# Layer 3 attention of a four-layer network: written order, one side piece per step, router on VectorE

## Chip, cores and metric

The kernel runs on one core of a Trainium2 chip, in fp32. The metric is the device time of one execution in microseconds. A core has TensorE (PE in the profile, its weight loads PEld), VectorE (DVE), ScalarE (ACT), GpSimd (POOL) and SyncE (SP, which issues most DMAs).

## What is computed

The network has four layers on x of shape [8, 256, 32, 32]. The change touches the third layer's attention and the routing of its mixture of experts (layers are counted from 0):

```python
# attention, per sample: N = 1024 tokens, D = 256, 8 heads of 32
qkv = layernorm(t) @ qkv_w.T + qkv_b
t2 = square(q @ k.T * 32**-0.5 + 5.0)
attn = t2 / sum(t2, axis=-1)
t = t + (attn @ v) @ proj_w.T + proj_b
# experts: 8 experts, each token goes to its best two
logits = layernorm(t) @ router_w.T
w, e = top_k(softmax(logits), 2); w = w / max(sum(w), 1e-12)
tokens = layernorm(t)
t = t + tokens + sum(w[i] * (gelu(tokens @ w1[e[i]] + b1[e[i]]) @ w2[e[i]] + b2[e[i]]) for i in (0, 1))
```

The denominators of the attention are had in closed form: the sum over m of (s_m + 5)^2 with s linear in k needs only the 32x32 matrix G = k k^T of a head (and the sum of k), then a product of G with q (Gq), a product with q and a sum over the head (D). Its inverse is Exp(-Ln(D)).

## The kernel before

Each layer is a generator; a layer's weights are loaded while the one before it still runs. Instructions are written in program order, and the compiler's tile scheduler then orders each engine's queue by priority and readiness. What is `pinned` keeps its place in program order. A pool with `bufs` buffers hands a tile out again when its last readers are done, and the first writer of the new tile waits for that.

`fast3` (attention) handles the 8 samples one after the other. For each one there are 32 steps (half of the queries, block of four heads, key tile of 128). A step does in TensorE four score products, one for each head of 32 channels, in four row strips of the array (L2686), into two PSUM tiles S of two banks each; in ScalarE two squares of 128x1024, from S to e (L2692); in TensorE the products of e with v of the step before (L2670), into the bank A. After 8 steps A times the inverse denominator goes to o (L2675), and after 16 the output projection of half a sample follows (L2681 adds it to x). PSUM has 8 banks: S has three buffers of two banks, A two buffers of one.

Beside the steps of sample b run, spread by `spread` over 33 calls: the routing of sample b-1 (`Routes.route`), and the norm, the transposes (xn), the projections q, k, v and the denominators of sample b+1. All these draw their PSUM from S as well (`pair`). In sample 0 `Routes.fill` also writes fill rows to the sorted lists in DRAM. `Routes.sort`, after each group of three samples, scatters rows by expert with GpSimd (L1026).

`Routes.route` normalizes the tokens (L1003 to L1019), stores them (L2390), adds them to x in GpSimd (L2391) and stores that too (L2392); transposes them on TensorE (L2398), takes the logits on TensorE (`mo_l`, 16 products with 8 columns), and then finds ranks, weights and places on VectorE. x has three buffers: that of sample b, of b+1, and of the one that is routed or loaded (L2570).

`fast3e` (experts) works on pairs of 128-row tiles. It first writes 16 half pairs beside the routing of the last sample:

```python
by_time([[0, 1, some(all_pairs, lead)], [1, 1.1, routing]])
```

In `by_time` each stream has a due time, a stride and a generator; the stream that is due first goes next.

Of the kernel before, what the change touches and what calls it, by code (L numbers as in the profile page):

```python
# [18 lines left out]
B = 8  # L19
# [878 lines left out]
class Fast:  # L898
# [123 lines left out]

    def scatter(self, group, after=(), **args):


        made = self.nc.gpsimd.indirect_dma_start(**args)  # L1026
        self.pinned(made)
        ins = made.ins
        self.tc.declare_no_dep(ins, group=group, reason="rows of their own")
        self.tc.add_to_no_dep_group(group, ins)  # L1030
        self.wait_for(ins, after)
        self.groups.setdefault(group, []).append(ins)
# [9 lines left out]
    def pinned(self, *ins):  # L1042
        for i in ins:
            self.tc.keep_in_program_order(i)

# [1263 lines left out]
class Routes:  # L2309
# [28 lines left out]
    def load(self, wp):  # L2338

        net, nc = self.net, self.net.nc  # L2340
        self.wr = net.load(wp, "l3f_wr", "(k p) o -> p k o", p=P)
# [17 lines left out]
    def fill(self):  # L2359
# [8 lines left out]
        for g, so in enumerate(self.sorteds):  # L2368
            self.fills[g] = []
            for lo in range(0, TILES[g], 26):  # L2370
# [5 lines left out]
                self.net.pinned(ins)  # L2376
# [3 lines left out]
    def route(self, b, x, ones, pair):  # L2380
# [8 lines left out]
        yield from net.token_norm_steps(xn, x, two)  # L2389
# [3 lines left out]
        yield  # L2393
        xk = ones.tile([P, KC, N], F32, tag="xn", name="mo_xk")
        for c in range(KC):
            ps = pair("mo_xT").rearrange("p h n -> p (h n)")
            for t in range(NT):
                nc.tensor.transpose(ps[:, bass.ts(t, P)], xn[:, t, bass.ts(c, P)], net.ident)  # L2398
            nc.vector.tensor_copy(xk[:, c, :], ps)
            yield  # L2400

        pr = two.tile([P, NT, E8], F32, tag="pr", name="pr")
        for t4 in range(0, NT, 4):
            ps = pair("mo_l")[:, 0]
            for i in range(4):
                net.linear(ps[:, bass.ts(i, E8)], xk, self.wr, bass.ts(t4 + i, P), slice(0, E8))
            nc.vector.tensor_copy(pr[:, t4 : t4 + 4], ps[:, : 4 * E8].rearrange("p (t e) -> p t e", e=E8))
            if not t4:
                yield
        red = two.tile([P, NT], F32, tag="red", name="red")  # L2410
        nc.vector.tensor_reduce(red, pr, AX.X, ALU.max)
        nc.vector.tensor_tensor(pr, pr, each(red), ALU.subtract)
        yield
# [11 lines left out]
        nc.vector.tensor_tensor(eq, other, mine, ALU.is_equal)  # L2425
        nc.vector.tensor_tensor(eq, eq, self.before.unsqueeze(1).to_broadcast([P, NT, E8, E8]), ALU.mult)
# [6 lines left out]
        for i in range(2):  # L2433
# [3 lines left out]
            nc.vector.tensor_reduce(weigh[:, i], tmp, AX.X, ALU.add)  # L2437
        nc.vector.tensor_tensor(red, weigh[:, 0], weigh[:, 1], ALU.add)
# [5 lines left out]
        yield  # L2444

        ps = pair("mo_n")[:, 0]
# [10 lines left out]
        for t in range(NT):  # L2457
            nc.vector.tensor_tensor(place[:, t], cnt[:, 0, t], carry, ALU.add)
            nc.vector.tensor_tensor(carry, carry, cnt[:, 1, t], ALU.add)
        yield  # L2460
# [59 lines left out]
def fast3(net, io):  # L2520
# [4 lines left out]
    with ExitStack() as ctx, ExitStack() as tok, ExitStack() as att, ExitStack() as bef:  # L2525
# [3 lines left out]
        def pair(name):  # L2529
            return net.lent["pair"](name) if not own else own["S"].tile([P, 2, HF], F32, tag="S", name=name)  # L2530

        def bank(name):
            return pair(name)[:, 0]
# [31 lines left out]
        xs, xns, qs, ks, vs, rs = ({} for _ in range(6))  # L2565

        def norm(b):
            x = xs[b] = xpool.tile([P, NT, C], F32, tag="x", name="x")

            (nc.sync if b else nc.scalar).dma_start(out=halves(x), in_=tokens(io.src[b]))  # L2570
            yield
            xt = one.tile([P, NT, C], F32, tag="xt", name="xt")
            yield from net.token_norm_steps(xt, x, norms, b > 0)
            yield
            xn = xns[b] = one.tile([P, KC, N], F32, tag="xn", name="xn")
            for c in range(KC):
                ps = pair("xn")
                for t in range(NT):
                    nc.tensor.transpose(ps[:, t // 4, bass.ts(t % 4, P)], xt[:, t, bass.ts(c, P)], net.ident)
                nc.vector.tensor_copy(xn[:, c, :], ps.rearrange("p h n -> p (h n)"))  # L2580
                yield
            nc.gpsimd.tensor_tensor(x, x, bo.unsqueeze(1).to_broadcast([P, NT, C]), ALU.add)

        def projections(b):
            xn = xns.pop(b)
            for d, w, bias, name in ((qs, wq, bq, "q"), (ks, wkk, bk, "k")):
                d[b] = own["two"].tile([P, KC, N], F32, tag=name, name=name)
                for c in range(KC):
                    ps = pair("qk")
                    for h in range(2):  # L2590
                        net.linear(ps[:, h], w, xn, bass.ts(c, P), bass.ts(h, HF))
                    nc.scalar.activation(d[b][:, c, :], ps.rearrange("p h n -> p (h n)"), AF.Identity, bias=bias(c))
                    yield
            v = vs[b] = own["two"].tile([P, NT, C], F32, tag="v", name="v")
            for t4 in range(0, NT, 4):
                ps = pair("v")
                for i in range(4):
                    net.linear(ps[:, i // 2, bass.ts(i % 2, C)], xn, wv, bass.ts(t4 + i, P), slice(0, C))
                nc.vector.tensor_copy(
                    v[:, t4 : t4 + 4].rearrange("p t c -> p (t c)"), ps.rearrange("p h n -> p (h n)")  # L2600
                )
                yield


            kt = own["k1"].tile([P, NT, KC, P + 4], F32, tag="kt", name="kt")
            nc.gpsimd.memset(kt[:, :, :, P], 1.0)
            for t4 in range(0, NT, 4):
                ps = pair("kT")
                for i in range(4):
                    for c in range(KC):  # L2610
                        nc.tensor.transpose(
                            ps[:, i // 2, (i % 2) * C + c * P : (i % 2) * C + (c + 1) * P],
                            ks[b][:, c, bass.ts(t4 + i, P)], net.ident,
                        )
                nc.vector.tensor_copy(
                    kt[:, t4 : t4 + 4, :, :P], ps.rearrange("p h (i c n) -> p (h i) c n", c=KC, n=P)
                )
                yield
            G = bank("G").rearrange("p (c n) -> p c n", c=KC)
            for c in range(KC):  # L2620
                for t in range(NT):
                    nc.tensor.matmul(
                        G[:, c, : P + 1], lhsT=kt[:, t, c, :P], rhs=kt[:, t, c, : P + 1],
                        start=(t == 0), stop=(t == NT - 1),
                    )
            gm = own["k2"].tile([P, KC, P + 4], F32, tag="gm", name="gm")
            nc.vector.tensor_tensor(gm[:, :, : P + 1], G[:, :, : P + 1], heads.to_broadcast([P, KC, P + 1]), ALU.mult)
            yield
            prod = one.tile([P, KC, N], F32, tag="xt", name="prod")
            r = rs[b] = own["two"].tile([P, KC, N], F32, tag="r", name="r")  # L2630
            for c in range(KC):
                ps = pair("Gq")
                for h in range(2):
                    nc.tensor.matmul(
                        ps[:, h], lhsT=gm[:, c, :P], rhs=qs[b][:, c, bass.ts(h, HF)], start=True, stop=True
                    )
                nc.vector.scalar_tensor_tensor(
                    prod[:, c, :], ps.rearrange("p h n -> p (h n)"), gm[:, c, P : P + 1], qs[b][:, c, :],
                    ALU.add, ALU.mult,
                )  # L2640
                yield
            for c in range(KC):
                ps = pair("D")
                for h in range(2):
                    nc.tensor.matmul(
# [592 lines left out]
```

## Time and profile before

| | us |
|---|---|
| median of 3 runs | 4171.47 (4164.15 to 4185.4) |
| profiled execution, its own time | 4178.96 |
| its span, first to last instruction | 4177.1 |
| attention of sample 0, first score product to the first one of the next sample (about) | 2819.65 to 2943 |
| attention of samples 1 to 6 | 2943 to 3708.8 |
| attention of sample 7 | 3708.8 to 3798.8 |
| experts, then checks of ranges | 3800 to 4177 |

Times in the trace count from the span's start. A row of the costliest groups gives line, engine, operation, tiles (out<-in), shape and count, then busy time and mean duration in ns, then the engine's idle time just before and what ended it. An fp32 product of TensorE leaves two records[...], so four heads are eight. Ends of TensorE's records overlap the next record's start.

### The profile page before, as it was taken

What the parts mean: (1) busy time and instruction counts of PE and PEld (TensorE: products, weight loads), DVE (VectorE), ACT (ScalarE), POOL (GpSimd) and SP (SyncE); (2) the same over time, 40 slices, a digit from 0 to 9 for tenths busy, and PEclk for the clock granted to TensorE, in tenths of its full rate; (3) what the DMA queues carried; (4) which work ended last, traced back from release to release, by engine and by line L of the source; (5) the groups of instructions that cost most, each with busy time, mean ns of one, the idle gap of its engine ahead of it and who ended that gap; (6) DMA issues with size and microseconds to landing.
All of it is one profiled execution on the core that took longest, in us unless ns stands there. A gap on an engine that the chain in (4) does not pass through costs nothing. (4 is left out here: it accounts for less than half of the span.)

```text
span 4177.1 us, 51736 instructions
## 1 busy us (share of the span) xinstructions
PE 3826.0 (92%) x19430; PEld 1887.8 (45%) x19430; DVE 2298.4 (55%) x3994; ACT 2260.1 (54%) x3030; POOL 566.3 (14%) x646
## 2 busy tenths in 40 slices
PE   8999999999878787789999969989899999999987
PEld 3323333333334444454444526653344444346986
DVE  2398798798896489942222356841232333324445
ACT  4556555555553367734334346516566556666554
POOL 0000000000000000000000013430000050124753
PEclk9999999999998889889999979999999999999998
DMA  3313223223131568720000013430700040136676
GB/s 100 113 43 124 90 73 120 88 74 109 62 107 47 185 246 291 264 73 21 21 21 29 22 56 109 142 121 11 219 31 31 9 145 31 37 111 195 202 233 219
DMA packets 210069, 441.13 MB, mean 106 GB/s; under 512 B 22281, under 2 KB 132828, under 8 KB 197396
## 3 DMA queue, kind: packets, MB, share of 16 engines
q1 hardware_dynamic: 186708, 386.17, 28.1%
q0 software_dynamic: 19440, 46.45, 3.3%
q10 hardware_dynamic: 3664, 5.11, 0.4%
q8 instruction: 157, 2.57, 0.3%
q14 instruction: 100, 0.82, 0.1%
HBM read 282.30 MB, written 162.28 MB: 106 GB/s over the span
## 5 line engine op out<-in xcount | busy, mean ns | idle before, releaser
L2692 ACT ACTIVATE e<-s,five 128x1024 f32<-128x1024 f32 x512 | 539.3, 1111 | 280.0 <-PE s L2686 279.2
L1249 DVE SCALAR_TENSOR_TENSOR a<-hp,w_f_vec,a 128x961 f32<-128x961 f32 (+1 forms) x496 | 608.7, 1233 | 115.3 <-ACT a L1242 106.7
L2686 PE MATMUL s<-q,k 32*128 32x512 f32 x2048 | 349.1, 644 | 16.3 <-ACT e L2692 12.1
L1401 ACT ACTIVATE e<-s 128x1024 f32<-128x1024 f32 x256 | 250.2, 1023 | 79.4 <-PE s L1395 62.8
L2670 PE MATMUL A<-e,v 128*32 128x512 f32 x2048 | 279.0, 609 | 0.0
L1355 DVE TENSOR_TENSOR sum<-sum,e 128x1024 f32<-128x1024 f32 x192 | 230.6, 1220 | 87.2 <-ACT e L1401 87.2
L78 PE MATMUL pi<-xn,w_l_wpi 128*128 128x512 f32 x512 | 249.0, 629 | 19.2 <-ACT v L1283 10.0
L1359 PE MATMUL A<-e,va 128*32 128x512 f32 x2048 | 263.0, 610 | 0.0
L2686 PEld LDWEIGHTS s<-q,k 32*128 32x128 f32 x2048 | 111.4, 184 | 179.4 <-issue 96.2
L1395 PE MATMUL s<-q,k 32*128 32x512 f32 x1024 | 181.2, 650 | 2.5 <-ACT e L1401 2.5
L78 PEld LDWEIGHTS pi<-xn,w_l_wpi 128*128 128x128 f32 x512 | 96.7, 199 | 161.9 <-issue 118.2
L2839 PE MATMUL h<-xk,w 128*128 128x128 f32 x1192 | 150.7, 281 | 19.0 <-DVE xk L2825 19.0
L1706 PE MATMUL acc<-wt,z 128*64 128x192 f32 (+4 forms) x1344 | 128.9, 334 | 42.4 <-DVE wt L1761 42.0
L1026 POOL DMA_INDIRECT res<-y,to x149 | 148.4, 996 | 106.6 <-DVE y L2863 47.7
L2839 PEld LDWEIGHTS h<-xk,w 128*128 128x128 f32 x1192 | 148.3, 197 | 24.1 <-DVE xk L2825 19.3
L2808 ACT COPY w<-w_l3f_w 128x512 f32 x149 | 92.6, 625 | 119.6 <-PE h L2839 116.3
L1440 ACT ACTIVATE hp<-pi,pib 128x512 f32<-128x512 f32 x128 | 87.2, 690 | 127.3 <-PE pi L78 127.2
L1310 POOL MEMSET thrice<- 32x128 f32 x32 | 6.3, 196 | 1021.7 <-PE pe L1326 1021.6
L2859 PE MATMUL y<-w_l3f_w,hid 128*128 x596 | 142.8, 382 | 0.3 <-ACT hid L2845 0.3
L1026 POOL DMA_INDIRECT so<-xl,rows x128 | 129.9, 1015 | 93.0 <-issue 51.0
L1706 PEld LDWEIGHTS acc<-wt,z 128*64 128x64 f32 x1344 | 97.7, 151 | 89.5 <-DVE wt L1761 60.1
L1359 PEld LDWEIGHTS A<-e,va 128*32 128x32 f32 x2048 | 57.6, 111 | 174.2 <-issue 172.9
(407 smaller groups left out, 6966.5 us busy)
## 6 DMA issues: line engine op xcount, KB each, us to landing
row<-shifts SPq DMA_DIRECT2D x144, 512.0 KB
x<-d SPq DMA_DIRECT2D x31, 1024.0 KB
xs<-so SPq DMA_DIRECT2D x73, 260.0 KB
so<-zero SPq DMA_DIRECT2D x5, 3380.0 KB
thrice<-vimg SPq DMA_DIRECT2D x64, 256.0 KB
gated<-st SPq DMA_DIRECT2D x32, 512.0 KB
hc<-gated SPq DMA_DIRECT2D x32, 512.0 KB
xl<-mox SPq DMA_DIRECT2D x64, 256.0 KB
```

The costliest lines, as they stand in the source:

```text
L78: self.nc.tensor.matmul(ps, lhsT=w[:, i, m], rhs=src[:, i, cols], start=(i == 0), stop=(i == k - 1))
L1026: made = self.nc.gpsimd.indirect_dma_start(**args)
L1249: nc.vector.scalar_tensor_tensor(to, fr, taps(t_), to, ALU.mult, ALU.add)
L1355: nc.vector.tensor_tensor(half, half, e[j], ALU.add)
L1359: nc.tensor.matmul(state["A"][32 * h : 32 * h + 32, c, :], lhsT=vas[b][:, kt, c, 32 * h : 32 * h + 32], rhs=e[h // 2][:, h % 2, :], start= ...
L1395: nc.tensor.matmul(ss[h // 2][:, h % 2], lhsT=ks[b][32 * h : 32 * h + 32, bass.ts(kt, P)], rhs=qs[b][32 * h : 32 * h + 32, bass.ts(gq, HF) ...
L1401: nc.scalar.activation(es[i][j], ss[j], AF.Exp, scale=SCALE)
L1706: nc.tensor.matmul(acc[o, a * IMG : e * IMG], lhsT=zs[b][:, c, t, :], rhs=wt[:, c, (a - lo) * IMG : (e - lo) * IMG], start=False, stop=(t ...
L2670: nc.tensor.matmul(A[32 * h : 32 * h + 32], lhsT=v[:, kt, c * P + 32 * h : c * P + 32 * h + 32], rhs=e[:, h, :], start=first, stop=last,)
L2686: nc.tensor.matmul(ss[h // 2][:, h % 2], lhsT=k[32 * h : 32 * h + 32, c, bass.ts(kt, P)], rhs=q[32 * h : 32 * h + 32, c, bass.ts(hh, HF)], ...
L2692: nc.scalar.activation(e[:, 2 * j : 2 * j + 2], ss[j], AF.Square, scale=SCALE, bias=five)
L2839: nc.tensor.matmul(ps[:, j, m], lhsT=ws[j][:, k, bass.ts(m, P)], rhs=xk[:, j, k], start=(k == 0), stop=(k == KC - 1),)
```

## The change

It does these things.

- S belongs to the scores alone. A has one buffer, and the freed bank X takes every other product of the loop, in pieces of one bank (`bank`). Evictions are of 128x512 instead of 128x1024.
- The four heads are issued in the order 2, 3, 0, 1 (`LATEST`).
- Attention runs over all 256 steps in one loop. `run(i, beside)` issues what is due in step i of routing, norms, loads, fills and sorts ahead of the values; after the values comes either half of an output projection or what is due of `parts` (projections, denominators, transposes).
- The due times are written by hand. The norm and the load of x run two samples ahead of the attention, the projections one.
- In the loop `in_order` adds, for TensorE, VectorE and ScalarE, a dependency from each instruction to the one before it on its engine, so that the queue is the written order.
- The router's logits come from VectorE: for each of 8 token tiles and 8 experts a product of 128x256 with a sum. The router's weights are for that copied to all partitions (`f3_wr`, 1 MB).
- Fill DMAs wait for the last square of their step (`anchor`).
- Before the loop, sample 1 is also normalized and transposed; behind it the last routing has stride 0.26.

The diff, cut to its core:

```diff
+    def token_norm_pieces(self, dst, x, pool):
...
+        for t in range(n):
+            nc.vector.bn_stats(st[:, t, :], x[:, t, :])
+            nc.vector.bn_aggr(mv[:, t, :], st[:, t, :])
+            if t % 2:
+                yield
+        yield
+        self.pinned(nc.scalar.activation(r[:, 0], mv[:, :, 1], AF.Ln, bias=self.eps5))
+        self.pinned(nc.scalar.activation(r[:, 0], r[:, 0], AF.Exp, scale=-0.5))
+        nc.vector.scalar_tensor_tensor(r[:, 1], mv[:, :, 0], -1.0, r[:, 0], ALU.mult, ALU.mult)
+        yield
+        for t in range(n):
+            nc.vector.tensor_scalar(dst[:, t, :], x[:, t, :], r[:, 0, t : t + 1], r[:, 1, t : t + 1], ALU.mult, ALU.add)
+            if t % 2:
+                yield
...
+    def in_order(self, *engines):
+        traced = self.nc.cur_bb.bb.instructions
+        start = len(traced)
+        yield
+        info = mybir.DependencyInfo(mybir.DependencyClass.NoSync, mybir.DependencyReason.DATA)
+        for engine in engines:
+            last = None
+            for i in traced[start:]:
+                if i.engine == engine:
+                    if last is not None:
+                        self.tc.add_manual_dep(i, last.name, info, reason="as planned")
+                    last = i
...
-        yield from net.token_norm_steps(xn, x, two)
+        yield from net.token_norm_pieces(xn, x, two)
         nc.sync.dma_start(out=self.normed[b], in_=xn)
         nc.gpsimd.tensor_tensor(x, x, xn, ALU.add)
         nc.sync.dma_start(out=self.sums[b], in_=x)
...
+        for t in range(NT):
+            for e in range(E8):
+                nc.vector.scalar_tensor_tensor(
+                    junk, xn[:, t, :], 1.0, self.wr[:, e, :], ALU.mult, ALU.mult, accum_out=pr[:, t, e : e + 1]
+                )
+                if e % 2:
+                    yield
...
+        def fetch(b):
+            x = xs[b] = xpool.tile([P, NT, C], F32, tag="x", name="x")
+            (nc.sync if b else nc.scalar).dma_start(out=halves(x), in_=tokens(io.src[b]))
...
+        def attention(beside, parts):
+            steps = [(b, hh, c, kt) for b in range(B) for hh in range(2) for c in range(KC) for kt in range(NT)]
...
+                if last:
+                    nc.vector.tensor_tensor(os[b][:, c, cols], A, rs[b][:, c, cols], ALU.mult)
+                    if c == KC - 1:
+                        projects.extend((i + 2 + t2 // 2, b, hh, t2) for t2 in (0, 2))
+            for i, (b, hh, c, kt) in enumerate(steps):
+                ss = [own["S"].tile([P, 2, HF], F32, tag="S", name="s") for _ in range(2)]
+                for h in LATEST:
+                    nc.tensor.matmul(
+                        ss[h // 2][:, h % 2], lhsT=ks[b][32 * h : 32 * h + 32, c, bass.ts(kt, P)],
+                        rhs=qs[b][32 * h : 32 * h + 32, c, bass.ts(hh, HF)], start=True, stop=True,
+                    )
+                e = es[i] = own["e"].tile([P, NH, HF], F32, tag="e", name="e")
+                for j in range(2):
+                    anchor[:] = [nc.scalar.activation(e[:, 2 * j : 2 * j + 2], ss[j], AF.Square, scale=SCALE, bias=five)]
+                run(i, beside)
+                if i:
+                    values(i - 1)
+                if projects and projects[0][0] <= i:
+                    project(*projects.pop(0)[1:])
+                    for d in parts:
+                        d[0] += d[0] <= i
+                else:
+                    run(i, parts)
+        LATEST = (2, 3, 0, 1)
+        STEPS, anchor = 4 * NT, []
+        def products(b):
+            yield from projections(b)
+            left = denominators(b)
+            for i, _ in enumerate(left):
+                yield
+                if b + 1 < B and 3 <= i < 7:
+                    turned(b + 1, (i - 3) // 2, (i - 3) % 2)
+                    yield
...
-        own["S"], own["A"] = io.pool(att, "f3s", 3, PSUM), io.pool(att, "f3v", 2, PSUM)
+        own["S"], own["A"] = io.pool(att, "f3s", 3, PSUM), io.pool(att, "f3v", 1, PSUM)
+        fetch(1)
...
+        own["X"] = io.pool(att, "f3o", 1, PSUM)
+        for b in range(B):
+            at = STEPS * b
+            if b + 1 < B:
+                parts.append([at + (3 if b else 0), 0.92, products(b + 1)])
+            if b + 2 < B:
+                beside.append([at + 8, 1, later(1, (fetch(n) for n in (b + 2,)))])
+                beside.append([at + 10, 0.5, norm(b + 2)])
+            if b:
+                beside.append([at + 3, 0.48, routed(b - 1)])
+            if b == 0:
+                beside.append([at + 10, 9, routes.fill(anchor)])
             if b == B - 1:
-                bef.close()
+                beside.append([at + 5, 2, loads()])
+        for g, (first, last) in enumerate(GROUPS[:-1]):
+            beside.append([STEPS * (last + 1), STEPS / (1 + NT * (last - first)), routes.sort(g)])
+        with net.in_order(mybir.EngineType.PE, mybir.EngineType.DVE, mybir.EngineType.Activation):
+            attention(beside, parts)
+        by_time(beside + parts)
...
-        by_time([[0, 1, some(all_pairs, lead)], [1, 1.1, routing]])
+        by_time([[0, 1, some(all_pairs, lead)], [1, 0.26, routing]])
...
+    d["f3_wr"] = np.tile(i["L3_ffn_router_w"].reshape(1, E8 * C), (P, 1))
```

## The prediction

> **What bounds the kernel now.** I first read busy time by engine and by slices on the page, then the costliest groups.
>
> ```profile
> span 4177.1 us, 51736 instructions
> PE 3826.0 (92%) x19430; PEld 1887.8 (45%) x19430; DVE 2298.4 (55%) x3994; ACT 2260.1 (54%) x3030; POOL 566.3 (14%) x646
> ...
> L2692 ACT ACTIVATE e<-s,five 128x1024 f32<-128x1024 f32 x512 | 539.3, 1111 | 280.0 <-PE s L2686 279.2
> ...
> L2686 PE MATMUL s<-q,k 32*128 32x512 f32 x2048 | 349.1, 644 | 16.3 <-ACT e L2692 12.1
> ...
> L2670 PE MATMUL A<-e,v 128*32 128x512 f32 x2048 | 279.0, 609 | 0.0
> ```
>
> The loop is the lines L2686, L2692 and L2670: 256 steps, 32 for each of 8 samples. ScalarE waits 279 us for scores, TensorE only 12 us for ScalarE, so TensorE is the bound. Busy time in stretches, of five steady samples (2 to 6), the last sample, and the first 46 us of the experts:
>
> ```profile
> core 0: us, PE busy (x) PEld busy (x) DVE busy (x) ACT busy (x) POOL busy (x), PEclk, DMA share, GB/s
> 3082.00:3708.80 626.80, 623.14 (x3703) 259.42 (x3703) 205.73 (x589) 383.24 (x385) 107.16 (x96) 1.00 0.16 54
> 3708.80:3798.80 90.00, 89.54 (x594) 33.09 (x594) 23.86 (x78) 69.97 (x71) 52.41 (x64) 0.98 0.53 161
> 3800.00:3846.00 46.00, 40.88 (x287) 37.74 (x288) 28.50 (x90) 26.34 (x58) 18.38 (x22) 0.96 0.70 241
> ```
>
> TensorE is busy 99% at full clock, VectorE 33%. A steady sample takes 626.8/5 = 125.4 us. What fills it shows TensorE's timeline (start, duration, line, count of records):
>
> ```profile
> 3105.01 1.46 PE L2686 MATMUL s<-q,k 32*128 32x512 f32 x8
> 3106.40 1.06 PE L2670 MATMUL A<-e,v 128*32 128x512 f32 x8
> 3107.40 1.23 PE L2686 MATMUL s<-q,k 32*128 32x512 f32 x8
> ...
> 3143.36 1.14 PE L2686 MATMUL s<-q,k 32*128 32x512 f32 x8
> 3144.43 1.07 PE L2670 MATMUL A<-e,v 128*32 128x512 f32 x8
> 3145.42 3.70 PE L78 MATMUL qk<-xn,w_l_wq 128*128 128x512 f32 x8
> ```
>
> I use distances from start to start, since ends overlap. A score group whose four heads run together takes 1.07 us (3143.36 to 3144.43), one that starts in two parts 1.39 (3105.01 to 3106.40) or up to 2; values take 0.99. Adding these distances over the 626.8 us gives, for each sample: scores 41.0 (1.28 a step), values 32.8, routing 6.4 (transposes 2.05, logits 3.76, counts 0.6), the rest 45.1 (q and k 14.5, v 7.3, transposes of x and of k 2.05 each, G 3.8, Gq and D 3.83 each, output projection 7.7).
>
> **What the Trainium skill says.** "TensorEngine Tiling (Array Packing)", Key Properties: tiles of the array run in parallel; the 1.07 us for four heads agrees. Its PSUM Bottleneck section says that eviction can become the bound after such a speedup. "Perfetto Trace Analysis", Matmuls: independent groups should rotate through PSUM banks so that an eviction overlaps the next group. That holds before (side work shares three pairs of banks with the scores) and no longer after, where it has one bank; no trace of before shows the cost. "TensorE: Matmul & The Clock Gate", Architectural detail: VectorE and ScalarE are strict queues, so an instruction that waits holds all behind it. The trace agrees: VectorE once stood 15.5 us for a load of x in sample 1, and TensorE lost 11.2 us there.
>
> **The change, part by part (per steady sample).**
>
> Scores. They own the three pairs, each step writes one group, and the heads of the later-freed pair come first, so that all four start together: 32 x 1.07 = 34.2 instead of 41.0, **-6.8**. Values unbroken: 32 x 0.99 = 31.7, **-1.1**.
>
> Router. 16 transposes and 16 logit products leave TensorE: 2.05 + 3.76, **-5.8**. VectorE gets 64 products with a sum. Layer 2 has the same form:
>
> ```profile
> 2435.82 0.42 DVE L2127 SCALAR_TENSOR_TENSOR junk<-xn,w_f_wr 128x256 f32<-128x256 f32 x1 [0.58 <-ACT xn L2115]
> 2436.17 0.08 DVE L2127 DVE_READ_ACCUMULATOR junk<-xn,w_f_wr 128x1 f32 x1
> 2436.36 0.42 DVE L2127 SCALAR_TENSOR_TENSOR junk<-xn,w_f_wr 128x256 f32<-128x256 f32 x1
> ```
>
> The pair repeats after 0.54 us, so 64 x 0.54 = 34 us more on VectorE, less two copies of 1.23 and two of 0.19: 41 + 34 - 3 = 72 of some 120 us. It is no bound in sum, but it is in places. TensorE's minimum is 125.4 - 13.7 = 111.7.
>
> Side work through one bank. A piece's eviction (0.69 for 128x512) lies behind the next step's scores and values, 2.06 us, and costs nothing while its engine is on time. I laid out the due times of the diff by hand and followed the queues of sample 3 with the durations above:
> - Step 3 has two pieces (last weights, first k). The second waits for ScalarE, which evicts only after its two squares (2 x 1.06): 1.0.
> - Steps 10 to 17. The x of two samples ahead takes the buffer of the sample being routed. Its norm is done about when step 8 starts; GpSimd's sum takes 4.5, the store 4, the load 4.2 (taken like the store):
>
> ```profile
> 3090.51 0.33 SPq L2390 DMA_DIRECT2D mox<-mo_x  x1
> 3095.13 0.33 SPq L2392 DMA_DIRECT2D mos<-x  x1
> 3099.04 0.32 SPq L2570 DMA_DIRECT2D x<-d  x1
> ```
>
>   These issues, each behind the last one's work, give 4.6 and 3.9. So x lands 12.8 us into step 8, but its statistics stand on VectorE's queue at step 10, 2 x 3.88 = 7.8 us in: VectorE stands 5. Behind it are the evictions of v (due in step 11) and then 4 statistics (0.5 with their aggregate) or 4 scalings (0.33) and 4 router products (2.1) a step. TensorE waits 0.5 + 0.6 for v, 2.9 where two k transposes share step 15, and 1.0 at step 17 for A, whose single buffer VectorE has not yet emptied: 5.0.
> - Steps 26 to 29. Five routing operations of 0.69 stand before the eviction ahead of Gq (1.5), 16 of 0.17 between two Gq pieces (1.6): 3.1.
> - A step without a piece is ScalarE's: first square's 1.06, then 0.06 + 1.23 until the next, 2.35 instead of 2.06: 0.3.
>
> Together 9.4, so 121.1. Sample 1 (fewer pieces left over) 119, sample 6 (no norm) 118.5, sample 0 (no routing, two projections later) 111, sample 7 32 x 2.35 + 4 x 2.0 = 83. Loop: 111 + 119 + 4 x 121.5 + 118.5 + 83 = 917.5.
>
> SyncE. Fills of 3.4 MB hold its queue some 11 us each (issues 11 apart in the trace); they now wait for a step's square. In sample 1 one ends as the routed rows are to be stored (+1), in sample 2 one stands before the load of x (+4). In sample 4 the sort's loads stand there too: the trace has x issued 12 us after the store, not 4 (+8). Loop 930.5; before, from 2819.65 to 3798.8, 979.2: **-48.7**.
>
> Ahead of the loop: the transposes of sample 1 (2.05) and halved evictions: **+4**. Weights for the router become 1 MB, as long as the store's 4 us, behind layer 2's tail (DMA share 0.39): 0, or +4 if that cover is gone.
>
> Behind it: the last sample's routing lies beside the first 8 pairs of experts, 3800 to 3846. VectorE then has norm 6.8 and its wait 1.5, products 34, the rest of routing 10.3, and for each pair 1.47: 8 x 1.47 = 11.8, in sum 64 us. Pairs later run at 3.95 us each and so need 32, the bound moves to VectorE: 64 - 46 = **+18** (+8 if the products slip behind the pairs, +25 if each pair waits its turn on VectorE).
>
> Sum: -48.7 + 4 + 18 = -26.7. The profiled execution had 4178.96, 7.5 above the median of the runs; against that median, 4171.5 - 26.7 = **4145**.
>
> **Bounds of what was not seen.** One bank: 0 (VectorE early) to 0.85 a piece (eviction bare), 31 pieces: 26 a sample; I take 9.4. Products: 0.35 if the read-out hid, 0.54; I take 0.54. Load of x: 4 to 12 (sample 4's case). Prologue -2 to +8.
>
> **Rivals.**
> - Everything hidden (0.17): statistics or scatters slip to where VectorE is idle. The loop loses the 9.4 of five samples and some 12 of SyncE, 59 us: 4086. For it: VectorE idle two fifths of a sample. Against: the three engines' order is fixed.
> - Slower (0.15): the x load decides. The store must wait for GpSimd, in samples 4 and 6 behind scatters, and VectorE's fixed queue passes each us on to TensorE. From 26.7/5 = 5.3 us later a sample the gain is gone; at 12, as the trace once shows, 5 x 12 = 60: 4205. For it: the 15.5 us stand of before. Against: that one lay behind 19 MB of fills, now spread.
> - No difference (0.13): the experts' start costs 30 and the prologue 8: 4161.
> - The groups stay broken (0.05): 7 x 6.8 = 48 comes back: 4193. Against: with the pieces, a step is longer than ScalarE's 2.12.
> - The forecast (0.5), 4115 to 4170.
>
> **Numbers.** What can be told from no change is 0.5%, 21 us. Faster: 0.17 + 0.42 of the forecast's 0.5, 0.01 more of the others: 0.60. Within: 0.24 (0.08 of the forecast, 0.13, some of the rest). Slower: 0.16. The range takes the hidden case and half of the slower one: 4085 to 4190.
>
> **What would show it.** Score groups of 1.07 throughout; ScalarE's idle before L2692 unchanged or more; VectorE near 60% in the loop and standing some 5 us at the statistics in samples 1 to 5; TensorE waiting on VectorE at v, k transposes and Gq; a loop of 930; the first 8 pairs in 64 us. Wrong would be score groups over 1.2, or VectorE's stand at the statistics over 10 us.

## The result and the profile after

The changed kernel is slower by 0.7%: 4201.1 us (median of 6 runs, 4187.89 to 4207.65) against 4169.27 for the kernel before (6 runs, 4162.21 to 4185.4), ratio 1.0067 with a 95% interval of 1.0041 to 1.0093. The forecast was 4145, with faster as the likeliest. The profiled execution took 4187.89, span 4186.2.

In the profiled execution layers 0 to 2, which the change does not touch, ended 22 us earlier than in that of before. So I compare by stretches, each measured from an event of its own trace: ahead of the loop (product for the bias `bo` to first score product), the loop (to the end of the last output projection), and the rest.

| us | before | forecast | after | difference | forecast of it |
|---|---|---|---|---|---|
| ahead of the loop | 50.1 | 54.1 | 71.1 | +21.0 | +4 |
| loop | 979.1 | 930.5 | 984.1 | +5.0 | -48.7 |
| loop's end to the last instruction | 378.4 | 396.4 | 383.2 | +4.8 | +18 |

The sum, +31, is what the medians show (+31.8). The loop's +5.0 is little more than two traces of one loop differ: run e2 below has the loop of after, and in its trace it lasts 980.2. The page of after, busy time and the costliest groups that answer to those of before:

```profile
span 4186.2 us, 52101 instructions
...
PE 3760.8 (90%) x19046; PEld 1815.2 (43%) x19046; DVE 2557.8 (61%) x5074; ACT 2273.4 (54%) x3078; POOL 569.0 (14%) x646
...
L2733 ACT ACTIVATE e<-s,five 128x1024 f32<-128x1024 f32 x512 | 542.4, 1111 | 314.3 <-PE s L2727 313.4
...
L2727 PE MATMUL s<-q,k 32*128 32x512 f32 x2048 | 314.5, 656 | 0.0
...
L2715 PE MATMUL A<-e,v 128*32 128x512 f32 x2048 | 279.0, 617 | 4.6 <-DVE o L2720 3.3
L2434 DVE SCALAR_TENSOR_TENSOR junk<-mo_x,w_f_wr 128x256 f32<-128x256 f32 x512 | 270.5, 528 | 12.3
```

TensorE is 65 us less busy in the whole program, and the scores 35 us less, so work has left TensorE. But the mean of a product on VectorE (L2434) is 528 ns where its usual duration is 424 (median): some are far longer. The stretches that were shown of before, now samples 2 to 6, sample 7 and the first 46 us of the experts:

```profile
core 0: us, PE busy (x) PEld busy (x) DVE busy (x) ACT busy (x) POOL busy (x), PEclk, DMA share, GB/s
3064.80:3705.80 641.00, 591.20 (x3451) 214.37 (x3450) 365.43 (x1231) 395.37 (x418) 97.91 (x87) 0.97 0.17 54
3705.80:3803.00 97.20, 91.61 (x576) 33.03 (x572) 61.58 (x237) 71.61 (x73) 58.59 (x71) 0.96 0.63 185
3803.00:3849.00 46.00, 41.88 (x280) 38.10 (x280) 35.53 (x116) 27.90 (x66) 21.42 (x26) 0.96 0.81 269
```

TensorE was busy 99% at clock 1.00; it is now busy 92% at 0.97. VectorE is at 57%, near the forecast 60, so it is no bound in sum. What TensorE waits for in the loop (engine and line, releaser: us in total, times, longest):

```profile
PE kT L2648 <- DVE kt L2651: 31.2, 8, 6.8
PE v L78 <- DVE v L2637: 12.3, 4, 7.6
PE Gq L2669 <- DVE prod L2670: 9.1, 6, 2.2
PE Gq L2669 <- DVE xn L2619: 6.1, 5, 1.2
PE qk L78 <- ACT r L2678: 4.1, 5, 0.8
PE A L2715 <- DVE o L2720: 3.3, 1, 3.3
```

All but the last two are waits for VectorE's evictions (its copies of results out of PSUM) of the one bank X. The first group explains itself in the timeline of step 15 of sample 3 (start, duration, engine, line):

```profile
3257.75 0.66 PE L2648 MATMUL kT<-ident,k 128*128 128x128 f32 x4
3258.81 4.55 POOL L2611 TENSOR_TENSOR x<-x,w_f_bo 128x2048 f32<-128x2048 f32 x1 [27.93 <-DVE xt L1040]
3259.05 4.59 DVE L2434 SCALAR_TENSOR_TENSOR junk<-mo_x,w_f_wr 128x256 f32<-128x256 f32 x1
3263.58 0.68 DVE L2651 COPY kt<-kT 128x512 f32<-128x512 f32 x1
3264.31 1.11 PE L2648 MATMUL kT<-ident,k 128*128 128x128 f32 x4 [5.91 <-DVE kt L2651]
3265.36 2.09 PE L2727 MATMUL s<-q,k 32*128 32x512 f32 x8
...
3267.38 1.67 PE L2715 MATMUL A<-e,v 128*32 128x512 f32 x8
```

GpSimd begins its sum of x and the bias at 3258.81. The router product that starts 0.24 us later takes 4.59 us instead of 0.42 and ends 0.28 us after the sum; the product that had started 0.22 us before the sum took its 0.42. The eviction of the first k transposes stands behind it, and TensorE waits 5.91 us for the bank. Then the score group takes 2.09 us and the values 1.67, where before showed 1.14 and 1.07. The granted clock says why (stretches of 3.4 us, PEclk is the third figure from the end):

```profile
3258.00:3261.50 3.50, 0.41 (x4) 0.17 (x2) 3.46 (x7) 1.01 (x2) 2.69 (x1) 1.00 0.00 0
3261.80:3265.20 3.40, 0.89 (x4) 0.71 (x4) 2.46 (x3) 0.00 (x0) 1.56 (x1) 0.50 0.00 0
3265.20:3268.60 3.40, 3.40 (x18) 0.72 (x16) 2.96 (x12) 1.09 (x2) 0.00 (x0) 0.50 0.00 0
3268.60:3272.00 3.40, 3.40 (x26) 1.23 (x23) 3.00 (x11) 2.20 (x4) 0.00 (x0) 0.99 0.00 0
```

In the whole loop the clock is 0.5 for 65 us, before for 24. From this I split a loop into three: **idle** time of TensorE (no record runs), **lost** time (half of what it was busy at half clock), and the rest, **work** at full clock.

| loop, us | length | work | idle | lost |
|---|---|---|---|---|
| before | 979.1 | 954.4 | 17.1 | 7.7 |
| after | 984.1 | 889.5 | 71.6 | 23.0 |
| e3, router back on TensorE | 978.4 | 932.2 | 40.2 | 6.1 |
| e5, sums on VectorE | 959.4 | 889.3 | 52.7 | 17.4 |
| e6, e5 and x later, xn early | 949.5 | 889.3 | 48.5 | 11.6 |
| e10, e6 and one piece a step | 923.4 | 889.8 | 31.9 | 1.7 |

The change took 65 us of work off TensorE and gave 55 back as idle time and 15 as clock.

### The profile page after: what moved, and what is told of

Same layout as the page of the kernel before. It is cut to its first block, busy times and chain, and to the rows that moved or that the text cites. A ratio compares the mean times of both kernels' runs of the same rounds, so it can differ in the third digit from the quotient of the medians.

```text
span 4186.2 us, 52101 instructions
## 1 busy us (share of the span) xinstructions
PE 3760.8 (90%) x19046; PEld 1815.2 (43%) x19046; DVE 2557.8 (61%) x5074; ACT 2273.4 (54%) x3078; POOL 569.0 (14%) x646
## 5 line engine op out<-in xcount | busy, mean ns | idle before, releaser
L2733 ACT ACTIVATE e<-s,five 128x1024 f32<-128x1024 f32 x512 | 542.4, 1111 | 314.3 <-PE s L2727 313.4
L2727 PE MATMUL s<-q,k 32*128 32x512 f32 x2048 | 314.5, 656 | 0.0
L2434 DVE SCALAR_TENSOR_TENSOR junk<-mo_x,w_f_wr 128x256 f32<-128x256 f32 x512 | 270.5, 528 | 12.3
L78 PE MATMUL pi<-xn,w_l_wpi 128*128 128x512 f32 x512 | 240.5, 611 | 14.8 <-ACT u L1538 9.2
L1431 PE MATMUL s<-q,k 32*128 32x512 f32 x1024 | 179.3, 648 | 2.4 <-ACT e L1437 2.4
L2727 PEld LDWEIGHTS s<-q,k 32*128 32x128 f32 x2048 | 92.2, 186 | 142.4 <-issue 136.2
L78 PE MATMUL v<-w_l_wv,xn 128*128 128x256 f32 x512 | 125.6, 394 | 12.4 <-DVE v L2637 12.3
```

The source lines that it names most:

```text
L78: self.nc.tensor.matmul(ps, lhsT=w[:, i, m], rhs=src[:, i, cols], start=(i == 0), stop=(i == k - 1))
L2434: nc.vector.scalar_tensor_tensor(junk, xn[:, t, :], 1.0, self.wr[:, e, :], ALU.mult, ALU.mult, accum_out=pr[:, t, e : e + 1])
L2727: nc.tensor.matmul(ss[h // 2][:, h % 2], lhsT=ks[b][32 * h : 32 * h + 32, c, bass.ts(kt, P)], rhs=qs[b][32 * h : 32 * h + 32, c, bass.ts(h ...
L2733: anchor[:] = [nc.scalar.activation(e[:, 2 * j : 2 * j + 2], ss[j], AF.Square, scale=SCALE, bias=five)]
```

## The theories

**A**: GpSimd's two sums a sample hold a router product on VectorE, and the clock falls behind the waits. **B**: x lands late and VectorE stands at its statistics. **C**: the new place of the transposed x makes the stretch ahead of the loop wait for layer 2. **D**, the rival: halved pieces, one bank and the fixed order cost themselves, whatever VectorE does. The runs used several chips, on which before takes 4164 to 4213 us; each kernel is compared by its ratio to before on its own chip, and in the trace by its stretches.

## First four runs

**e1, the meetings moved apart.**

```diff
         def norm(b):
...
+            if b < 2:
+                biased(b)
+        def biased(b):
             nc.gpsimd.tensor_tensor(xs[b], xs[b], bo..., ALU.add)
...
+            if b > 1:
+                beside.append([at + 1, 1, (biased(n) for n in (b,))])
# route, behind the sum of x and xn on GpSimd:
+        for _ in range(3):
+            yield
```

> The changed kernel with its two large GpSimd sums of a sample moved away from the router's products on VectorE: the bias is added at step 1 of the sample's own attention, and three more due times (1.44 steps) lie between the routing's sum and the first product. Nothing else moves. Theory A (a product of two SBUF operands on VectorE stands until a running GpSimd sum is over, 4.6 us twice a sample, and TensorE's waits behind it [...]halve its clock): no product over 0.6 us, TensorE's 6.6 us wait between the two k transposes of step 15 falls to 3 or less, the half-clock stretches after it vanish, the loop loses 25 to 40 us: about 4168 (ratio to before 0.999). Theory B (one bank and VectorE's added load make the waits, the meeting with GpSimd is beside the point): less than 8 us gained, about 4197 (1.006).

Measured: 1.0051 (1.0035 to 1.0068), loop 971.1. The meeting with routing's sum is gone, the other is not:

```profile
3299.22 4.55 POOL L2617 TENSOR_TENSOR x<-x,w_f_bo 128x2048 f32<-128x2048 f32 x1 [27.73 <-DVE xt L1040]
3299.46 4.59 DVE L2436 SCALAR_TENSOR_TENSOR junk<-mo_x,w_f_wr 128x256 f32<-128x256 f32 x1
```

GpSimd is not among the engines of `in_order`; the scheduler starts the sum as soon as its data are there, wherever it was written. So the run tests half of A only: its loop is 13 us shorter than that of after, 9 shorter than that of e2.

**e2, the transposed x of sample 0 in the third x buffer.**

```diff
         def turned(b, h, c):
-            if b not in xns:
+            if b not in xns and not b:
+                first = xpool.tile([P, NT, C], F32, tag="x", name="xn")
+                xns[b] = first.rearrange("p t c -> p (t c)").rearrange("p (k n) -> p k n", k=KC)
+            elif b not in xns:
```

> The changed kernel with the transposed tokens of sample 0 in the third buffer of x, which is free until the loop, instead of a pool that opens only where layer 2's space is given back. Theory C (ahead of the loop 21 us are lost because the first evictions stand behind layer 2's last gathers): from the bias product to the first score product 71 us become about 52, the loop stays, in sum -19: about 4182 (1.003). Rival (layer 2's tail sets the start anyway, by VectorE or by another tile): 71 stays, 4201.

Measured: 1.0045 (1.0028 to 1.0061); ahead of the loop 53.8 instead of 71.1. TensorE's timeline of after, where the fourth bank of transposes waits 17 us for an eviction:

```profile
2763.14 0.80 PE L2618 MATMUL xn<-ident,xt 128*128 128x128 f32 x2 [2.49 <-DVE xt L1040]
2781.17 1.12 PE L2618 MATMUL xn<-ident,xt 128*128 128x128 f32 x4 [17.23 <-DVE xn L2619]
```

and of e2, where it does not:

```profile
2794.27 2.04 PE L2621 MATMUL xn<-ident,xt 128*128 128x128 f32 x6 [2.49 <-DVE xt L1040]
2796.10 4.38 PE L78 MATMUL qk<-xn,w_l_wk 128*128 128x512 f32 x6
```

C holds. In the change, xn lies in a pool that opens behind `HOLD` (the mark from which a layer needs the space of the one before it), and VectorE's queue has its first evictions behind layer 2's last sums, which wait for gathers; before, it lay in a pool opened earlier. VectorE's timeline of after:

```profile
2780.03 0.48 DVE L2278 SCALAR_TENSOR_TENSOR s<-yg,m,s 128x256 f32<-128x256 f32 x1 [0.59 <-DMA yg<-pk,idx]
2780.43 2.58 DVE L2619 COPY xn<-xn 128x512 f32<-128x512 f32 x4
```

The ratio fell by 0.0022, where 17 us are 0.0041; after and e2 were timed on different occasions, and their intervals overlap.

**e3, the router's transposes and logits back on TensorE**, through the bank X.

```diff
-        for t in range(NT):
-            for e in range(E8):
-                nc.vector.scalar_tensor_tensor(junk, xn[:, t, :], 1.0, self.wr[:, e, :], ALU.mult, ALU.mult, accum_out=...)
+        for c in range(KC):
+            for h in range(2):
+                ps = bank("mo_xT")   # 4 transposes, a copy, 4 yields
...
+        for t4 in range(0, NT, 4):
+            ps = bank("mo_l")        # 4 linears, a copy, 8 yields
```

> The changed kernel with the router's logits back on TensorE: 16 transposes and 16 products of 8 columns a sample, in pieces through the bank X beside the steps, in place of 64 products on VectorE; due times otherwise as they were. Theory A and theory B both: no long stand of VectorE, a steady sample near 121 us (111.7 + 6 of router work + 3 of waits) instead of 130, loop -45, experts' start -5: about 4150 (0.995). Rival D (the pieces of one bank and the fixed order cost this by themselves): a steady sample stays at 130 or more, 4200 or over.

Measured: 1.0044 (1.0028 to 1.0060), loop 978.4. Samples 2 to 5 take 125 to 135, in the mean 128, far from the 121 of A and B and near D's 130, though no product is left that could be held. By the table, TensorE has 43 us of work more than in after (6.1 for each of 7 samples), and idle and lost time fall by 31 and 17. So in this form the router's move gains nothing in the loop: it saves 43 us of work and costs 48.

**e4, without `in_order`** (the scheduler orders the queues).

```diff
-        with net.in_order(mybir.EngineType.PE, mybir.EngineType.DVE, mybir.EngineType.Activation):
-            attention(beside, parts)
+        attention(beside, parts)
```

> The changed kernel without the added dependencies: the scheduler orders TensorE, VectorE and ScalarE in the loop by itself. Theory A: the scheduler does not know of the stand, the products meet the sums as before, score groups break in part: within 10 us of the changed kernel, 4190 to 4210. Rival E (the fixed order is what lets a standing VectorE hold the evictions): evictions move ahead of products, -25 us or more, 4175 (1.001).

Measured: 1.0276 (1.0259 to 1.0293), loop 1058.5. Neither expectation foresaw that: one was no change from after, the other a gain. The written order is worth 74 us of loop here. TensorE's waits in the middle samples:

```profile
PE A L2715 <- DVE o L2720: 46.0, 5, 9.5
PE v L78 <- DVE v L2637: 33.3, 8, 10.7
```

Once in each sample A waits some 9 us for the eviction of o, and v for its own: VectorE's queue has another order there. Which priority would mend that was not tried.

## A against D

**e5, both sums on VectorE**, in pieces of two token tiles.

```diff
     def token_norm_pieces(self, dst, x, pool, plus=False):
...
             if t % 2:
+                if plus:
+                    nc.vector.tensor_tensor(x[:, t - 1 : t + 1], x[:, t - 1 : t + 1], dst[:, t - 1 : t + 1], ALU.add)
                 yield
# route
-        nc.gpsimd.tensor_tensor(x, x, xn, ALU.add)
# norm, for samples 2 to 7
-            nc.gpsimd.tensor_tensor(xs[b], xs[b], bo..., ALU.add)
+                beside.append([at + 31, 1, biased(b + 2)])   # the same on VectorE, 4 pieces
```

> Changed kernel, with both 128x2048 sums of GpSimd in the loop (x plus the normalized tokens, x plus the bias) made on VectorE instead, in four pieces of 128x512 each: the first ones beside the scalings of routing's norm, the bias ones in steps 31 to 34. So no router product can meet a GpSimd sum. Theory A (the loop's missing gain is router products held 4.6 us by GpSimd's sums, and the half clock that follows each long wait): the second k transpose of step 15 waits under 2 us instead of 6.6, half-clock stretches fall from 65 us to under 30 (the waits for x in samples 1 and 4 stay), middle samples take 122 to 124 instead of 128 to 134, loop 945 to 955, ratio to before 0.995 to 1.000. Theory D (the halved pieces, one bank and the fixed order cost themselves): middle samples stay at 127 or more, loop 970 or more, ratio 1.003 to 1.007.

Measured: 1.0014 (1.0001 to 1.0027), loop 959.4, 24.7 less than after. None of the 512 products takes over 0.50 us (up to 5.19 in after). TensorE's waits in the loop:

```profile
PE kT L2656 <- DVE kt L2659: 14.5, 8, 2.8
PE v L78 <- DVE v L2645: 11.3, 3, 5.0
PE Gq L2677 <- DVE prod L2678: 9.2, 6, 2.2
```

The wait at the k transposes is 14.5 where after had 31.2; half clock falls from 65 to 37.5 us. A is shown, for nearly half of what the loop missed (53.6 us). D keeps a part: the length lies between the two expectations, and samples 1 to 5 still take 123 to 129.

**e6, e5 with x later and xn early** (the edit of e2, and:)

```diff
-                beside.append([at + 10, 0.5, norm(b + 2)])
+                beside.append([at + (13 if b else 10), 0.5, norm(b + 2)])
```

> The kernel of e5 with two more edits: sample 0's transposed x lies in the third x buffer, so that the prologue does not wait for layer 2's tail (-17 us, as in e2), and from sample 1 on the norm of two samples ahead starts at step 13 instead of 10, 11.6 us later, so that x has landed. Theory A with the wait for x: VectorE stands under 1 us at the statistics in samples 1, 2, 3, 5 and at most 5 in sample 4, half clock under 15 us, loop 930 to 940, ratio 0.988 to 0.993: faster than both kernels. Theory D: loop 965 or more, ratio 0.998 to 1.002.

Measured: 0.9946 (0.9928 to 0.9963): faster than both kernels. No stand of over 0.7 us at the statistics is left, but the loop takes 949.5, 10 less than in e5 and not 930 to 940: the waits at the double pieces are all there (kT 14.5, Gq 15.3).

**e12, the late norm alone** in the changed kernel (the same line).

> The changed kernel with one edit: from sample 1 on the norm of two samples ahead starts at step 13 instead of 10. The stands of VectorE at the statistics (8.1, 5.4, 4.8, 12.2 and 4.5 us in samples 1 to 5) go, all but some 4 us in sample 4; GpSimd's bias sum moves three steps with the norm and meets router products there as before. If x's landing time costs what e6 suggests beside e5: loop 970 to 977, ratio 1.003 to 1.005. If the stands were only cover for work that VectorE had to do anyway behind them: loop 980 to 988, ratio 1.006 to 1.008.

Measured: 1.0016 (0.9999 to 1.0033), loop 968.2, 15.9 less than after, as B expects, rather more. The waits for v are gone; those of kT move (14.5 on its own eviction, 10.3 on that of a projection). GpSimd's sum of x and the bias moves with the norm: 13 products are held as in after, but none any more at the two k pieces of step 15. So e12 alone does not part B from A; e6 against e5, where nothing is held, gives the later norm 10 us.

**e10, e6 with one piece in a step.**

```diff
-                parts.append([at + (3 if b else 0), 0.92, products(b + 1)])
+                parts.append([at + (5 if b else 0), 1, products(b + 1)])
```

> The kernel of e6 with one edit: the pieces of projections and denominators start at step 5 of a sample instead of 3 and come one per step (stride 1 instead of 0.92), so that no step has two v, k-transpose, G or Gq pieces; the last four (D) then lie in steps 5 to 9 of the next sample, beside its first k pieces. In e6 the steps with two pieces, 15 and 29, take 5.1 to 6.5 and 7.05 us. If two pieces in one step are what is left of the one-bank cost: step 15 takes 3.9 and step 29 at most 4, samples 2 to 5 take 119 to 121, loop 920 to 930, ratio 0.989 to 0.991. If VectorE's queue is late there anyway, so that the wait only moves to other steps, or if A's eviction now waits for D: samples stay at 123 to 126, loop 945 to 955, ratio 0.994 to 0.997.

Measured: 0.9909 (0.9883 to 0.9935), loop 923.4, ahead of the loop 54.0, as its first case forecasts: the best kernel of the study. The five steady samples run at clock 1.00, 120.6 us each:

```profile
3058.10:3661.00 602.90, 578.85 (x3455) 210.70 (x3454) 357.10 (x1274) 393.69 (x415) 57.06 (x78) 1.00 0.17 56
```

What is left of TensorE's waits in the loop:

```profile
PE qk L78 <- ACT r L2689: 14.0, 15, 1.2
PE A L2726 <- DVE o L2731: 10.5, 7, 3.1
PE Gq L2680 <- DVE xn L2630: 2.8, 5, 0.6
...
PE kT L2659 <- DVE kt L2662: 0.7, 1, 0.7
```

The double steps are now 5 to 7, with the last pieces of the denominators (D) and the first of k, whose evictions are ScalarE's: 0.9 us each, not 2 to 6.

**e11, one piece in a step alone**, in the changed kernel.

> The changed kernel with one edit, that of e10 (pieces from step 5, one per step); GpSimd's sums, the early norm and the prologue stay as changed. If the parts add up (e10 took 26 us of loop from e6): loop 955 to 962, ratio about 1.000 to 1.002, and half clock still over 30 us, since the held products remain. If a hold of 4.6 us hurts only where two pieces meet behind it[...]: loop 935 to 945, half clock under 25 us, ratio 0.996 to 0.998.

Measured: 0.9997 (0.9986 to 1.0008), loop 946.5, half clock 27: between the two. Its timeline shows what a held product costs where one piece stands behind it:

```profile
3272.51 4.63 DVE L2434 SCALAR_TENSOR_TENSOR junk<-mo_x,w_f_wr 128x256 f32<-128x256 f32 x1
3277.07 0.68 DVE L2637 COPY v<-v 128x512 f32<-128x512 f32 x1
...
3277.80 3.14 PE L78 MATMUL v<-w_l_wv,xn 128*128 128x256 f32 x8 [2.54 <-DVE v L2637]
```

TensorE's next v piece comes after 2.54 us idle, instead of 5.91 with two pieces. Alone, the three loop edits bring 24.7 (sums), 15.9 (norm) and 37.6 (pieces), in sum 78; together (e10, with e2's) 60.7. They overlap, probably because each shortens waits in which the others meet; that was not taken apart.

## Parts of the change in the kernel before

**e7, only the order of the heads.**

```diff
-                for h in range(NH):
+                for h in (2, 3, 0, 1):
```

> The kernel before with one edit: the four score heads of a step are issued in the order 2, 3, 0, 1. If the broken groups (1.28 us a step) come from the order alone, groups become whole (1.07 to 1.1), and the loop goes from 979 to 930 to 950, ratio 0.990 to 0.995. If they come from side work that shares the three pairs, or if a whole group only starts as late as its last pair is free, so that TensorE waits in front of it instead of inside it: loop 970 to 985, ratio 0.998 to 1.002.

Measured: 1.0001 (0.9987 to 1.0015), loop 979.3. The order alone does nothing there, so the whole groups come from S being the scores' own, from the written order, or from both. The trace of e4, which has the first without the second, goes part of the way: of the 128 steps of samples 2 to 5, the four heads start more than 0.7 us apart in 48 before, in 19 in e4 and in 9 in after.

**e8, only the router on VectorE**, and **e9, its products in smaller portions.** The weights come for each sample into the buffer of the transposed tokens.

```diff
+        wr = ones.tile([P, KC, N], F32, tag="xn", name="wr")...
+        nc.sync.dma_start(out=wr, in_=self.wr)
+        for t in range(NT):
+            for e in range(E8):
+                nc.vector.scalar_tensor_tensor(junk, xn[:, t, :], 1.0, wr[:, e, :], ALU.mult, ALU.mult, accum_out=...)
# e8: a yield every 16 products, ROUTE = 12; e9: every 4 products, ROUTE = 25
```

> The kernel before with the router's logits on VectorE (64 products of 128x256 with a sum for each sample, beside the scheduler's own order), and nothing else of the change; the weights are loaded for each sample into the buffer of the transposed tokens. If the 5.8 us of TensorE are hidden as forecast: samples 2 to 6 take 119 to 120 instead of 125.4, loop 940 to 950, ratio 0.991 to 0.996 with the experts' start 10 longer. If products held by GpSimd's sums (4.6 us each) delay the evictions: no gain or a loss, loop 975 to 1000, ratio 1.000 to 1.008.

> The kernel of e8 (before, with the router's logits on VectorE) with its 64 products issued in 16 portions of four instead of four of sixteen, so that the scheduler's program order has 25 calls of routing in 33 instead of 12. In e8 ScalarE's queue stood 22 us a sample at routing's Exp, which waits for the last product, with the squares behind it, and TensorE waited 20 us for them. If that was the portions: the stand falls under 5 us, samples 2 to 6 take 121 to 128, loop 950 to 1000, ratio 0.995 to 1.005. If VectorE's products do not fit beside the scheduler's own order at all: the stand stays over 15 us, loop 1060 or more, ratio over 1.02.

Measured: e8 1.0261 (1.0219 to 1.0302), loop 1081.9; e9 1.0114 (1.0083 to 1.0144), loop 1005.3. ScalarE's waits at routing's Exp in the middle samples of e8, and what TensorE then waits for:

```profile
ACT pr L2409 <- DVE pr L2407: 113.1, 5, 22.7
```

```profile
PE s L2681 <- ACT e L2687: 108.5, 5, 21.8
```

and of e9:

```profile
ACT pr L2409 <- DVE pr L2407: 27.3, 5, 6.7
```

The Exp is pinned, waits for the last product, and the squares queue behind it: a stand that both of my theories for e8 missed. Spread, it falls to 5.5 us a sample, and the loop is still 26 us longer than before: 27 less of work, 29 more of idle and 23 more of lost time. Both kernels also hold one product a sample for 4.6 us. In the two placements that were tried, the router's move does not pay in the scheduler's order. In the written order it should pay in e10: its loop of 923.4 is shorter than the work alone of e3, 932.2. That is an estimate; e10 with the router on TensorE was not run.

## The prediction, step by step

1. **Scores -6.8.** A group behind a piece takes 1.07 as forecast, one in a step without a piece about 1.4. By distances, samples 2 to 5 need 36.0 a sample, not 34.2, but 1.5 of that is the half clock. Their work at full clock is 34.5, before 40.6: this term was nearly right.
2. **Values -1.1.** They take 37.0 in after, behind waits and at half clock, and 32.7 in e10, as before: nothing gained.
3. **Router -5.8.** TensorE lost that work. The products' own price was set a little high (0.47 us in a row, forecast 0.54). **Here the prediction failed**: it bounded a product by 0.35 to 0.54 and never asked what GpSimd does meanwhile, although it names the sum and its 4.5 us. In the loop of after 12 products take 4.6 to 5.2 us. Behind four of them, held by the bias sum where two k pieces share a step, TensorE waits 5.9 to 6.8 us, and without any (e5) the loop is 24.7 us shorter. The Trainium skill, "SBUF — State Buffer", section "SBUF: two separate sides", says that VectorE and GpSimd share a pair of ports as an exclusive lock, and that a VectorE operation with two SBUF inputs takes part in it against a GpSimd operation that reads SBUF, as this sum does. The trace agrees: 4.59 against 0.42.
4. **One bank, 9.4.** The places and most sizes were right: Gq 15.2 us in the loop (5 x 3.1 = 15.5), step 3's second piece 4.1 (5 x 1.0), and the k transposes 14.5 (5 x 2.9 = 14.5) once no product is held; with the holds 31.2. (The forecast's own sum gives 121.1 a sample, and it went on with 121.5.) Idle time was 71.6 in all. The forecast contains about 66: its 930.5 less the work of step 6. That the two are near is luck: 19 of the 71.6 go with the holds, which it did not know (e5: 52.7), and part of what it did expect did not come.
5. **No clock term.** The sum ran at full clock. 23 us went that way, before 7.7. The Trainium skill, "TensorE: Matmul & The Clock Gate", section on HAM oscillation, warns of idle gaps over about 3.4 us. Here shorter ones count too: each of the eleven idle times of over 1.8 us in the loop of after, 2.2 to 7.6 long, has a stretch of 3.4 to 10.2 us at 0.5 with it; in other runs some had none (last section).
6. **Work under-counted.** The forecast's own numbers make about 864 us of work (111 for sample 0, 111.7 for six, 83 for sample 7); measured 889.5. Samples 2 to 5 have 115.1 each. Each piece added by halving costs 0.1 (k: 8 pieces 7.66, before 4 pieces 7.26; q the same), 2.9 a sample with v, the transposes, G, Gq and D, for which the forecast has nothing; scores and values are the other 0.6. Sample 7 was set at 83 in all and has 88.9 of work (97 with its waits): only four of the six projection pieces in it were counted.
7. **Load of x.** VectorE stood 8.1, 5.4, 4.8, 12.2 and 4.5 us in samples 1 to 5; forecast 5, in sample 4 8 more. The two named:

```profile
3240.17 0.43 DVE L1030 BATCH_NORM_STATS2 tn_s<-x 128x6 f32<-128x256 f32 x1 [4.77 <-DMA x<-d]
...
3376.87 0.43 DVE L1030 BATCH_NORM_STATS2 tn_s<-x 128x6 f32<-128x256 f32 x1 [12.15 <-DMA x<-d]
```

   The slower rival rested on this and named 4205, close to the measurement, but for the wrong reason: e6 puts the load at 10 us of loop, e12 at 16 at most, while A and the doubles weigh more.
8. **Ahead of the loop +4.** e2's 53.8 is that +4; the 17 of C were missing. I had looked for a late DMA there, not for a buffer's pool.
9. **Experts +18.** It was +4.8. VectorE's sum of 64 us was right (the last product ends at 3865.6, 62.6 after the loop), but the pairs did not wait for it: the eleventh copy xk (which runs two pairs ahead) starts 45.3 us after the loop's end, before the change 52.0. That is the case called "products slip behind the pairs", at less than its price. One execution of each kernel is a thin base for it: in the other traces, taken on several chips, this stretch lasts 374 to 383 us (e3, e5 to e8) or 397 to 405 (e1, e2, e4, e9 to e12), so what the router's move costs there stays open.

Of the signs it named, score groups of 1.07 behind a piece, ScalarE's idle time before its squares (314.3, before 280.0), VectorE's share, the stands and the three waits came; the loop and the experts' start did not. Of its signs of being wrong, score groups over 1.2 stayed few (11 of 124 in samples 2 to 5), and the stand of over 10 us came once, in sample 4, where its own sum had 13.

Of the 53.6 us that the loop missed, 5 are idle time beyond the forecast's 66, 23 the clock, and 25 step 6. By cause, the held products of step 3 are 24.7 (19 idle and 6 clock, by e5) and step 6 is 25; the clock behind other waits is 17, against 13 of forecast waits that did not come. Outside the loop, step 8 adds 17 and step 9 takes 13 back. So four terms failed: the price of a router product beside GpSimd, the clock, which was put at nothing, the work of halved pieces, and the buffer ahead of the loop.

## What to carry over

When work moves to VectorE, price it against what GpSimd runs beside it, not only against VectorE's idle time: one GpSimd sum of 4.6 us can hold one product, all evictions behind it, and TensorE. Where TensorE has one bank for side work, avoid two pieces that VectorE evicts in one step: one in a step took 26 us off the loop of e6 and 38 off that of after. Beside a wait of about 2 us or more, allow for the clock too: a stretch of 3.4 us at half clock, which often came with it here, costs 1.7. A saving of TensorE work counts only where what stands around it (who sums, when a load is awaited, how pieces are spaced) keeps it from becoming idle time: with the same 65 us less work, e10 takes 0.9% less time than before and the change 0.7% more.

## What the runs showed of the hardware that I had not expected

- A 128x256 product with two SBUF inputs on VectorE that meets a GpSimd sum of 128x2048 takes 4.6 us, until the sum ends, instead of 0.42; with both sums on VectorE (e5) none of 512 takes over 0.50.
- The granted clock fell behind waits shorter than expected, and not behind all: 2.2 us in after and twice 1.74 in e5 had a stretch at 0.5 behind them, while three waits of 2.2 in e5 and one of 3.10 in e6 had none. So these traces give no sharp length.
- Without a written order the same instructions took 74 us more of loop (e4).
